# A fused RWKV attention and mixture-of-experts block: reordered first part, blends split between VectorE and ScalarE, one token table, row gathers three steps ahead

## The chip, the cores and the metric

The kernel runs on one core of a Trainium2 chip. The metric is the device time of one execution in microseconds (us). Beside the timed runs there is one profiled execution, whose trace gives the times of single instructions. The engines are called TensorE (PE in the profile; PEld are its weight loads), VectorE (DVE), ScalarE (ACT), GpSimd (POOL) and SyncE (SP). SyncE only issues DMAs here; GpSimd issues the indirect DMAs, which gather and scatter rows by index.

## The reference

The input x is 2 x 2048 tokens of 256 channels, fp32. It is normalised once, and two branches are added to it:

```python
xn  = layernorm(x)
out = x + attention(xn) + experts(xn)

def attention(x):                      # RWKV
    x = layernorm(x) * ln_g + ln_b
    last = x shifted by one token (0 ahead of the first)
    k = (x*mix_k + last*(1-mix_k)) @ Wk.T        # v, r alike
    num, den = num*td + exp(k)*v, den*td + exp(k)     # along time
    return (sigmoid(r) * num/(den + 1e-8)) @ Wo.T

def experts(x):                        # 8 experts, the best 2 of each token
    scores = relu(x @ Wr + br)
    w = softmax over the two best scores
    h = relu(x @ W1[e] + b1[e])        # 256 -> 1024
    return sum over the two of w[e] * (h @ W2[e] + b2[e])
```

## The kernel before, in words

The 4096 tokens are cut into 8 blocks of 512 (four to each batch row), a block into four tiles of 128 tokens. Everything after line 356 is written in the order in which each engine shall do it (`tc.manual_schedule()`), so the order of the calls in the source is the order of every engine's queue. Pools still decide when a buffer is free: `ps_a`, `ps_t`, `ps_h` and `ps_y` are PSUM pools of two buffers each.

*First part, lines 357 to 467.* For each block b, `stats(b)` (L180) computes mean and variance on VectorE and the reciprocal deviations on GpSimd (a power); `normed(b)` (L211) writes the normalised block x2, three quarters on VectorE and one on ScalarE, and SyncE stores it in a table in DRAM from which tokens are gathered later; `turned(b)` (L226) transposes the block on TensorE, and ScalarE evacuates each of the two channel halves twice, as x2T for the router and as xaT, scaled and shifted by ln_g and ln_b, for the attention. `scored(b)` (L246) multiplies by the router's weights, ScalarE copies the result out, and `routed(b)` (L259) transposes it into `sps`. `mix(n)` takes the next n blends from a generator (L266): once for a block VectorE computes dx = now - last, and then for k, v and r two instructions (one for each channel half) dx*mix + last. `some(n)` takes the next n of 48 projection outputs from another generator (L290): each is a 128x512 result of two fp32 matrix products in a `ps_a` buffer, which the profile shows as four matmul records, and ScalarE evacuates it into `kvr` (L304). `divisors` (L199) is another power on GpSimd.

*Routing, lines 468 to 695.* `best_two` (L336) finds the two experts of each token on VectorE. Two matmuls with ones and an upper triangle give prefix counts (`pre`, L482). A chain of small VectorE instructions (L497 to L554) turns these into a slot number for each token and expert, `pos`. There are 71 units of 128 slots; 64 of them form 32 pairs, 7 are single. The slots of one unit belong to one expert. To find the token of each slot, the positions are split into low and high parts, and for 8 chunks of 8 columns VectorE builds one-hot tables (L652 to L673): `oh_a` for the low part, `oh_b` for the high part, and `oh_t`, which is `oh_b` times the token's number less 2048. TensorE multiplies `oh_a` with both others, 16 matmuls a chunk, so that `inv` holds for each slot whether it is taken, and by which token. L683 to L692 turn this into two index tables: `frm`, the row to gather, and `into`, the row to scatter to, with empty slots sent to rows behind the last token. `experts_of_places` (L602) works out for each of 39 places (pairs and singles) which expert's weights it needs (`whose_i`), and the table `mine` for the gates. Between these steps `mix` and `some` calls are laid, so that TensorE has projections to do.

*Experts, lines 858 to 906.* There are 37 steps; each handles one place. `gather(s)` (L789) fetches the rows of its tokens, by one GpSimd DMA for each unit; `unnorm(s)` (L800) undoes a scaling of the rows and computes the gates; `turn(s)` (L814) transposes the rows; `first_product(s)` (L823) computes the 8 hidden chunks `hp`, with relu on ScalarE; `second_product(s, hs, i)` (L839) computes `yp`, adds the bias, multiplies by the gate, and scatters the result with an adding DMA on GpSimd. Weights are loaded by SyncE with expert numbers from `whose_i` (L773, L781). In step s the kernel issues the weights of steps s+1 and s+2, the gather of step s+2, then the first product of s, a part of the attention (`scans`, `gated`, `attended`), the transposes of s+1, the second product of s, and unnorm of s+2. The first 12 steps (SW = 12) add into a buffer `acc`, which starts as a copy of x; at the end of the twelfth, SyncE copies `acc` to the output (L906), and the remaining 25 steps add into the output itself. A last stage (L909 on) for two rare units runs only if they are needed.

Of the kernel before, what the change touches and what calls it, by code (L numbers as in the profile page):

```python
# [9 lines left out]
F32 = mybir.dt.float32  # L10
# [16 lines left out]
def rwkv_moe_block(  # L27
# [21 lines left out]
    nc = tc.nc  # L49
# [130 lines left out]
    def stats(b):  # L180
        def mk(nm, shape):
            return rpool.tile(shape, F32, bufs=1, name=f"{nm}_{b}")

        st = mk("st", [P, NS, 6])
        mv = mk("mv", [P, NS, 2])
        for i in range(NS):
            nc.vector.bn_stats(st[:, i, :], xts[b][:, i, :])
            nc.vector.bn_aggr(mv[:, i, :], st[:, i, :])
        mean, var = mv[:, :, 0], mv[:, :, 1]

        at = ts(b, NS)
        w = mk("w", [P, NS])
        nc.gpsimd.tensor_scalar(w, var, 1.0 + LN_EPS, LN_EPS * LN_EPS, ALU.mult, ALU.add)
        rrs[b] = rr_all[:, at]
        nc.gpsimd.tensor_tensor(rrs[b], w, power[:, 0:NS], ALU.pow)
        nc.gpsimd.tensor_scalar(ve_all[:, at], var, LN_EPS, 0.0, ALU.add, ALU.add)
        mrrs[b] = (mean, mk("mrr", [P, NS]))
# [28 lines left out]
    def turned(b):  # L226
        x2 = x2s[b]
        x2T = x2Ts[b] = rpool.tile([P, NC, TB], F32, tag="x2T", name=f"x2T_{b}")

        xaT = xaTs[b] = xa_pool.tile([P, NC, TB + 1], F32, name=f"xaT_{b}")  # L230
        if b % BPS == 0:
            nc.gpsimd.memset(xaT[:, :, 0:1], 0.0)
        else:
            nc.gpsimd.tensor_copy(xaT[:, :, 0:1], xaTs[b - 1][:, :, TB : TB + 1])
        for c in range(NC):
            tp = ps_t.tile([P, TB], F32, tag="pt", name=f"tp_{b}_{c}")
            for t in range(NS):
                nc.tensor.transpose(tp[:, ts(t, P)], x2[:, t, ts(c, P)], ident)
            nc.scalar.copy(x2T[:, c, :], tp)
            nc.scalar.activation(  # L240
                xaT[:, c, 1 : TB + 1], tp, AF.Identity, bias=vec(5, c), scale=vec(4, c)
            )

# [20 lines left out]
    blends = [[] for _ in range(NB)]  # L264

    def blender():  # L266
        for b in range(NB):
            now, last = xaTs[b][:, :, 1 : TB + 1], xaTs[b][:, :, 0:TB]

            dx = mixes.tile([P, NC, TB], F32, tag="dx", bufs=1, name=f"dx_{b}")  # L270
            nc.vector.tensor_tensor(dx, now, last, ALU.subtract)
            for i in range(3):
                m = mixes.tile([P, NC, TB], F32, tag="mix", name=f"mix{i}_{b}")
                for c in range(NC):
                    nc.vector.scalar_tensor_tensor(  # L275
                        m[:, c, :], dx[:, c, :], vec(1 + i, c), last[:, c, :],
                        ALU.mult, ALU.add,
                    )
                blends[b].append(m)
                yield  # L280
# [8 lines left out]

    def pieces():  # L290
        for b in range(NB):
            pool = kvr_pool if b < NB // 2 else kvr_late
            kvr[b] = pool.tile([P, 3, NC, TB], F32, tag="kvr", name=f"kvr_{b}")
            for i, (w, f, sign) in enumerate(
                ((wk_sb, AF.Exp, 1.0), (wv_sb, AF.Copy, 1.0), (wrr_sb, AF.Exp, -1.0))
            ):
                for o in range(NC):
                    m = blends[b][i]
                    p = ps_a.tile([P, TB], F32, tag="pa", name=f"p{i}_{b}_{o}")
                    for c in range(NC):  # L300
                        nc.tensor.matmul(  # L301
                            p, w[:, c, ts(o, P)], m[:, c, :], start=(c == 0), stop=(c == NC - 1)
                        )
                    nc.scalar.activation(kvr[b][:, i, o, :], p, f, scale=sign)  # L304
                    yield
# [50 lines left out]
    order = ctx.enter_context(tc.manual_schedule())  # L356
    stats(0)
    colp = ps_t.tile([P, n_rows], F32, tag="pt", name="colp")
# [10 lines left out]
    stats(1)  # L369
    normed(0)  # L370
    turned(0)


# [28 lines left out]
    token = count("token", NT, F16, base=-NTOK // 2, step=P, chan=1)  # L402
# [15 lines left out]
    stats(2)  # L418
    normed(1)
    scored(0)  # L420
    turned(1)
    nc.scalar.activation(td, cols[:, E * NH : E * NH + NC], AF.Exp)
    mix(3)
    routed(0)
    scored(1)
    normed(2)
    some(2)
    turned(2)
    routed(1)
    stats(3)  # L430
    stats(4)
    normed(3)
    some(2)
    scored(2)
    turned(3)
    divisors(0)
    routed(2)
    mix(3)
    some(2)
    scored(3)  # L440
    routed(3)
    stats(5)
    normed(4)
    some(2)
    turned(4)
    stats(6)
    normed(5)
    some(1)
    scored(4)
    turned(5)  # L450
    stats(7)
    normed(6)
    routed(4)
    some(1)
    scored(5)
    turned(6)
    divisors(1)
    normed(7)
    routed(5)
    some(1)  # L460
    scored(6)
    turned(7)
    mix(3)
    routed(6)
    some(1)
    scored(7)
    routed(7)
# [11 lines left out]
    some(4)  # L479
# [14 lines left out]
    some(2)  # L494
# [54 lines left out]
    )  # L549
    pos = rt("pos", (P, E, NT))  # L550
# [4 lines left out]
    some(6)  # L555
    mix(3)
    some(6)
    mix(1)

# [22 lines left out]
    mix(2)  # L582
# [18 lines left out]

    def experts_of_places():  # L602
# [15 lines left out]
        whose = rt("whose", (P, NW))  # L618
# [15 lines left out]
        nc.vector.tensor_copy(whose_i, whose)  # L634
        last = rt("last", (P, 2))
# [14 lines left out]
    inv = ps_y.tile([P, 2 * NU], F32, tag="py", name="inv")  # L650
    opool = routing.enter_context(tc.tile_pool(name="opool", bufs=3))
    for i0 in range(0, K * NT, CH):  # L652

        tables = []
        for nm, n, src, ramp2 in (("a", P, lo, lo_iota), ("b", NU, hi, hi_iota)):
            t = opool.tile([P, CH // 2, n, 2], F16, tag=f"oh_{nm}", name=f"oh_{nm}_{i0}")
            nc.vector.tensor_tensor(
                t,
                ramp2.unsqueeze(1).to_broadcast([P, CH // 2, n, 2]),
                src[:, i0 : i0 + CH].rearrange("p (a b) -> p a b", b=2).unsqueeze(2)  # L660
                .to_broadcast([P, CH // 2, n, 2]),
                ALU.is_equal,
            )
            tables.append(t)
        a, bq = tables
        bt_ = opool.tile([P, CH // 2, NU, 2], F16, tag="oh_t", name=f"oh_t_{i0}")
        t0 = i0 % NT
        nc.vector.tensor_tensor(
            bt_, bq,
            token[:, t0 : t0 + CH].rearrange("p (a b) -> p a b", b=2).unsqueeze(2)  # L670
            .to_broadcast([P, CH // 2, NU, 2]),
            ALU.mult,
        )  # L673
        mix((0, 0, 0, 1, 0, 1, 0, 2)[i0 // CH])
        for i in range(CH):
            for j, right in enumerate((bq, bt_)):
                nc.tensor.matmul(
                    inv[:, j * NU : (j + 1) * NU], a[:, i // 2, :, i % 2],
                    right[:, i // 2, :, i % 2],
                    start=(i0 + i == 0 and j == 0), stop=(i0 + i == K * NT - 1 and j == 1),  # L680
                )
        some((1, 1, 1, 1, 1, 2, 1, 0)[i0 // CH])
    invs = rt("invs", (P, 2, NU))  # L683
    nc.vector.tensor_copy(invs, inv.rearrange("p (a u) -> p a u", a=2))
    empty = rt("empty", (P, NU))
    nc.vector.tensor_tensor(empty, invs[:, 0, :], less, ALU.mult)
    row = rt("row", (P, NU))
    nc.vector.tensor_tensor(row, invs[:, 1, :], empty, ALU.subtract)
    into = const.tile([P, NU], I32, name="into")
    nc.vector.tensor_tensor(into, row, rest_row, ALU.add)  # L690
    frm = const.tile([P, NU], I32, name="frm")
    nc.vector.tensor_scalar_min(frm, into, float(NTOK - 1))  # L692
    mix(2)
    experts_of_places()
    routing.close()
    gpool = ctx.enter_context(tc.tile_pool(name="gpool", bufs=3, side="right"))
# [103 lines left out]
    def unnorm(s):  # L800

        gates[s] = []
        for i, g in enumerate(rows_of[s]):
            nc.vector.tensor_scalar(  # L804
                g[:, 0:C], g[:, 0:C], g[:, C + E : C + E + 1], None, ALU.mult
            )
        for i, g in enumerate(rows_of[s]):
            gm = small.tile([P, E], F32, tag=f"gm{i}", name=f"gm_{s}_{i}")
            nc.vector.tensor_tensor(gm, g[:, C : C + E], mine[:, seq[s], :], ALU.mult)
            gate = small.tile([P, 1], F32, tag=f"gate{i}", bufs=3, name=f"gate_{s}_{i}")  # L810
            nc.vector.tensor_reduce(gate, gm, AX.X, ALU.add)
            gates[s].append(gate)
# [26 lines left out]
    def second_product(s, hs, i):  # L839
# [7 lines left out]
        y = gpool.tile([P, C], F32, tag="y", bufs=5, name=f"y_{s}_{i}")  # L847
        nc.vector.tensor_tensor(y, yp, b2_sb, ALU.add)  # L848
        nc.vector.tensor_scalar(y, y, gates[s][i], None, ALU.mult)  # L849
# [9 lines left out]
    gather(1)  # L859
    load_first(0)  # L860
    load_second(0)
    load_first(1)
    some(6)
    unnorm(0)
    turn(0)
    some(2)
    unnorm(1)
    projecting.close()
    a1 = ctx.enter_context(tc.tile_pool(name="a1", bufs=1))
    hpool = ctx.enter_context(tc.tile_pool(name="hpool", bufs=2 * NH))  # L870
    turns = 0
    for s in range(NSTEP):
# [5 lines left out]
        if s + 2 < NSTEP:  # L878
            gather(s + 2)
# [13 lines left out]
        if b < NB:  # L893
            gated(b, o)
        adds = [second_product(s, hs, i) for i in range(len(units(seq[s])))]
# [5 lines left out]
        if s + 2 < NSTEP:  # L901
            unnorm(s + 2)
        if s == SW - 1:
# [9 lines left out]
    with tc.If(taken > 0):  # L913
# [6 lines left out]
        for s in range(NSTEP, NW):  # L920
# [3 lines left out]
            unnorm(s)  # L924
            turn(s)
# [42 lines left out]
```

## Time and profile before

| what | us |
|---|---|
| three timed runs | 665.69 to 669.6, median 667.3 |
| the profiled execution | 669.53 |
| its span, first to last instruction | 667.7 |
| TensorE busy | 637.4 (95%) |
| VectorE busy | 344.6 (52%) |
| ScalarE busy | 212.6 (32%) |
| GpSimd busy | 237.1 (36%) |
| first projection starts | 16.86 |
| last transpose of scores | 50.85 |
| first expert product starts | 123.04 |

A group row of the profile gives the line, engine, operation and tiles (result, then sources), the number of instructions; then busy time in us and the mean duration of one in ns; then the idle time ahead of them on their engine and what ended most of it. A timeline row gives start and duration in us, and in brackets the idle time before it with its releaser. Rows of digits are the span in 40 equal slices, in tenths; PEclk is the clock granted to TensorE in tenths of full speed. A SyncE row such as `117.85 0.40 SPq ... w` is the issue of a weight load, which lands some microseconds later (a median of 8.3 for the 1 MB loads).

### The profile page before, as it was taken

The page shows a single profiled execution, that of the slowest core. Times are in us where ns is not written, and L with a number is a line of the kernel's source. Part 1 is how long each engine was busy: PE and PEld are TensorE (multiplying, and loading weights), DVE is VectorE, ACT ScalarE, POOL GpSimd, SP SyncE. Part 2 cuts the span into 40 slices and gives each one's busy share as a digit, 9 for nine tenths or more (in the row PEclk, how much of TensorE's full clock was granted, in tenths as well). Part 3 has the DMA queues.
Part 4 walks back from the last instruction along what each step waited for, and adds up shares of the span by engine and source line. Part 5 has one row for each costly group of instructions (what it writes and reads, how often), then busy time and mean ns, then how long its engine had stood idle before and what let it go on. Part 6 is the DMA issues. An engine that isn't in the chain of part 4 may idle for free. (4 is left out here: it accounts for less than half of the span.)

```text
span 667.7 us, 9123 instructions
## 1 busy us (share of the span) xinstructions
PE 637.4 (95%) x3077; PEld 500.5 (75%) x3077; DVE 344.6 (52%) x779; ACT 212.6 (32%) x444; POOL 237.1 (36%) x206
## 2 busy tenths in 40 slices
PE   4999999899999999999989999999999999999993
PEld 2454454688888888887878888888888888888882
DVE  8988998446545547765587666422222121222110
ACT  4683323323332333332323333322223222222320
POOL 5551103034343354404355334343434433434211
PEclk9999999999999999999989999999999999999997
DMA  8548101876887886799677777777566776566621
GB/s 268 176 129 268 16 1 43 287 227 212 251 231 219 230 263 194 184 309 283 151 160 214 193 204 182 216 168 222 168 175 182 218 207 217 168 174 189 212 29 17
DMA packets 92408, 124.50 MB, mean 186 GB/s; under 512 B 15452, under 2 KB 80552, under 8 KB 92232
## 3 DMA queue, kind: packets, MB, share of 16 engines
q1 hardware_dynamic: 74368, 100.99, 46.3%
q0 software_dynamic: 17472, 22.86, 18.2%
q8 instruction: 25, 0.41, 0.3%
q14 instruction: 23, 0.19, 0.1%
q10 hardware_dynamic: 520, 0.05, 0.1%
HBM read 105.89 MB, written 26.38 MB: 198 GB/s over the span
## 5 line engine op out<-in xcount | busy, mean ns | idle before, releaser
L831 PE MATMUL hp<-xT,w 128*128 128x256 f32 (+1 forms) x1184 | 252.1, 369 | 2.3 <-DMA w<-in_L_ffn_W_dram 1.5
L835 ACT ACTIVATE h<-hp,b 128x256 f32<-128x256 f32 (+1 forms) x296 | 135.9, 459 | 349.2 <-PE hp L831 256.5
L844 PE MATMUL yp<-w,h 128*128 128x256 f32 x1104 | 246.1, 381 | 0.0
L831 PEld LDWEIGHTS hp<-xT,w 128*128 128x128 f32 x1184 | 199.2, 190 | 50.8 <-ACT h L835 16.6
L844 PEld LDWEIGHTS yp<-w,h 128*128 128x128 f32 x1104 | 208.6, 192 | 26.7
L853 POOL DMA_INDIRECT out_dram<-y,into x50 | 82.6, 1652 | 206.7 <-DVE y L849 129.5
L821 DVE COPY xT<-xp 128x512 f32<-128x512 f32 (+1 forms) x37 | 24.2, 655 | 148.2 <-PE xp L819 148.2
L793 POOL DMA_INDIRECT xg<-table,frm x69 | 77.8, 1127 | 55.7 <-DVE mix L275 34.9
L848 DVE TENSOR_TENSOR y<-yp,b 128x256 f32<-128x256 f32 x69 | 29.2, 423 | 115.3 <-PE yp L844 115.3
L853 POOL DMA_INDIRECT acc<-y,into x19 | 31.3, 1648 | 87.6 <-DVE y L849 51.2
L732 DVE RECIPROCAL dn<-dn 128x512 f32<-128x512 f32 x16 | 53.6, 3353 | 0.5
L304 ACT ACTIVATE kvr<-p 128x512 f32<-128x512 f32 x48 | 28.7, 599 | 54.9 <-PE p L301 54.9
L804 DVE TENSOR_SCALAR xg<-xg 128x256 f32<-128x256 f32 x69 | 22.3, 359 | 26.2 <-DMA xg<-table,frm 26.2
L275 DVE SCALAR_TENSOR_TENSOR mix<-dx,cols,xaT 128x512 f32<-128x512 f32 x48 | 33.3, 756 | 0.4
L301 PE MATMUL p<-mix,wk 128*128 128x512 f32 x64 | 30.4, 617 | 0.5 <-DVE mix L275 0.5
L301 PE MATMUL p<-mix,wv 128*128 128x512 f32 x64 | 29.5, 596 | 0.0
L301 PE MATMUL p<-mix,wr 128*128 128x512 f32 x64 | 29.3, 596 | 0.0
L741 PE MATMUL op<-wo,z 128*128 128x256 f32 x128 | 29.1, 380 | 0.0
L741 PEld LDWEIGHTS op<-wo,z 128*128 128x128 f32 x128 | 24.3, 190 | 3.6 <-ACT o_sb L744 0.3
L849 DVE TENSOR_SCALAR y<-y,gate 128x256 f32<-128x256 f32 x69 | 25.4, 369 | 2.4
L819 PE MATMUL xp<-ident,xg 128*128 128x128 f32 x138 | 21.7, 275 | 4.2 <-DVE xg L804 3.2
L819 PEld LDWEIGHTS xp<-ident,xg 128*128 128x128 f32 x138 | 17.0, 141 | 9.2 <-issue 1.9
(168 smaller groups left out, 365.4 us busy)
## 6 DMA issues: line engine op xcount, KB each, us to landing
w<-in_L_ffn_W_dram SPq DMA_DIRECT2D x74, 1024.0 KB, 8.3
b<-in_L_ffn_b_dram SPq DMA_DIRECT2D x37, 128.0 KB, 3.8
table<-x SPq DMA_DIRECT2D x8, 512.0 KB, 3.0
x<-in_L_attn_x_dram SPq DMA_DIRECT2D x7, 512.0 KB, 4.6
out_dram<-o_sb POOLq DMA_DIRECT2D x5, 512.0 KB, 6.1
acc<-o_sb POOLq DMA_DIRECT2D x3, 512.0 KB, 6.1
xg<-table,frm POOLq DMA_INDIRECT x69, 6.8
out_dram<-y,into POOLq DMA_INDIRECT x50, 6.7
```

Of the source, the lines that this page charges most:

```text
L275: nc.vector.scalar_tensor_tensor(m[:, c, :], dx[:, c, :], vec(1 + i, c), last[:, c, :], ALU.mult, ALU.add,)
L301: nc.tensor.matmul(p, w[:, c, ts(o, P)], m[:, c, :], start=(c == 0), stop=(c == NC - 1))
L304: nc.scalar.activation(kvr[b][:, i, o, :], p, f, scale=sign)
L732: nc.vector.reciprocal(dn, dn)
L741: nc.tensor.matmul(op, z[:, c, ts(t, P)], wo_sb[:, c, :], start=(c == 0), stop=(c == NC - 1))
L793: nc.gpsimd.indirect_dma_start(out=g, out_offset=None, in_=table, in_offset=bass.IndirectOffsetOnAxis(ap=frm[:, u : u + 1], axis=0), bound ...
L819: nc.tensor.transpose(xp[:, c, ts(i, P)], g[:, ts(c, P)], ident)
L831: nc.tensor.matmul(hp, w1_sb[:, c, ts(j, P)], xT[:, c, :], start=(c == 0), stop=(c == NC - 1))
L835: nc.scalar.activation(h[:, 0:n], hp, AF.Relu, bias=b1_sb[:, j : j + 1])
L844: nc.tensor.matmul(yp, hs[j][:, ts(i, P)], w2_sb[:, j, :], start=(j == 0), stop=(j == NH - 1))
L848: nc.vector.tensor_tensor(y, yp, b2_sb, ALU.add)
L853: return nc.gpsimd.indirect_dma_start(out=to, out_offset=bass.IndirectOffsetOnAxis(ap=into[:, u : u + 1], axis=0), in_=y, in_offset=None, ...
```

## The change

It has four parts.

*First part.* `stats` can be done for some of the four tiles. 25 matmuls of a 128x512 bf16 tile of zeros are put into TensorE's order (13, 4 and 8, `keep_warm`). `normed(0)` moves up, ahead of the transpose of the small vectors; block 0's evacuations change order (xaT before x2T) and its dx is taken in two halves. The calls of stats, normed, turned, scored, routed, mix and some are ordered anew; 15 projection outputs stand before the last transpose of scores, where 12 stood.

*Blends.* For blocks 3 to 7, ScalarE computes m = last*(1 - mix), one channel half after each projection output from the thirteenth on, and VectorE then does now*mix + m; these five blocks have no dx. A small table `unmixed` holds 1 - mix.

*One table of tokens.* The token's number is stored with an offset that keeps it from being zero: numbers 0 to 2047 as -2048 to -1, numbers 2048 to 4095 as 1 to 2048. So `oh_a` times `oh_t` alone tells empty slots (zero) from taken ones; each chunk has 8 matmuls instead of 16. `experts_of_places` moves ahead of the blends that followed `frm`, with its last part split off as `experts_later`; projections are laid between them, and `some(6)` before `unnorm(0)` becomes `some(4)`.

*Experts.* Three gathers are issued before the loop and gather(s+3) in step s; the rows have four buffers instead of three, and y has a pool of its own. The gates are split from `unnorm`. In the last step, the bias times the gate is prepared, and one VectorE instruction reads `yp`, multiplies and adds.

The core of the diff, with the reordered calls of the first part cut to their beginning:

```diff
@@ blends
+    NDX = 3
+    ahead = []
+
+    def preparer():
+
+        for b in range(NDX, NB):
+            for i in range(3):
+                m = mixes.tile([P, NC, TB], F32, tag="mix", name=f"mix{i}_{b}")
+                for c in range(NC):
+                    nc.scalar.activation(
+                        m[:, c, :], xaTs[b][:, c, 0:TB], AF.Copy, scale=unmixed[:, i, c : c + 1]
+                    )
+                    if c == NC - 1:
+                        ahead.append(m)
+                    yield
...
-            dx = mixes.tile([P, NC, TB], F32, tag="dx", bufs=1, name=f"dx_{b}")
-            nc.vector.tensor_tensor(dx, now, last, ALU.subtract)
+            if b < NDX:
+
+                dx = mixes.tile([P, NC, TB], F32, tag="dx", bufs=1, name=f"dx_{b}")
+                for c in (slice(0, 1), slice(1, NC)) if b == 0 else (slice(0, NC),):
+                    nc.vector.tensor_tensor(dx[:, c, :], now[:, c, :], last[:, c, :], ALU.subtract)
...
+                    by, other = dx, last
+                else:
+                    m = ahead.pop(0)
+                    by, other = now, m
                 for c in range(NC):
                     nc.vector.scalar_tensor_tensor(
-                        m[:, c, :], dx[:, c, :], vec(1 + i, c), last[:, c, :],
+                        m[:, c, :], by[:, c, :], vec(1 + i, c), other[:, c, :],
                         ALU.mult, ALU.add,
@@ pieces()
                     nc.scalar.activation(kvr[b][:, i, o, :], p, f, scale=sign)
+                    done += 1
+                    if done > NFIRST:
+                        next(preparing, None)
                     yield
@@ first part
+    keep_warm(13)
     stats(0)
+    stats(1, 0, 2)
+    normed(0)
...
-    stats(1)
-    normed(0)
+    stats(1, 2, NS)
+    keep_warm(4)
     turned(0)
...
+    mix(1)
...
-    stats(2)
     normed(1)
-    scored(0)
+    keep_warm(8)
+    some(2)
     turned(1)
@@ one-hot chunks
-            for j, right in enumerate((bq, bt_)):
-                nc.tensor.matmul(
-                    inv[:, j * NU : (j + 1) * NU], a[:, i // 2, :, i % 2],
-                    right[:, i // 2, :, i % 2],
-                    start=(i0 + i == 0 and j == 0), stop=(i0 + i == K * NT - 1 and j == 1),
-                )
-        some((1, 1, 1, 1, 1, 2, 1, 0)[i0 // CH])
+            nc.tensor.matmul(
+                inv, a[:, i // 2, :, i % 2], bt_[:, i // 2, :, i % 2],
+                start=(i0 + i == 0), stop=(i0 + i == K * NT - 1),
+            )
+        some(SOME[i0 // CH])
...
     nc.vector.tensor_scalar_min(frm, into, float(NTOK - 1))
+    experts_of_places()
     mix(2)
-    experts_of_places()
+    some(2)
+    mix(1)
+    some(2)
+    mix(1)
+    experts_later()
     routing.close()
-    gpool = ctx.enter_context(tc.tile_pool(name="gpool", bufs=3, side="right"))
+    gpool = ctx.enter_context(tc.tile_pool(name="gpool", bufs=4, side="right"))
@@ second_product()
+        y = ypool.tile([P, C], F32, tag="y", name=f"y_{s}_{i}")
+        if s == NSTEP - 1:
+            nc.vector.scalar_tensor_tensor(y, yp, gates[s][i], b2g[i], ALU.mult, ALU.add)
+        else:
+            nc.vector.tensor_tensor(y, yp, b2_sb, ALU.add)
+            nc.vector.tensor_scalar(y, y, gates[s][i], None, ALU.mult)
@@ experts
     gather(0)
     gather(1)
+    gather(2)
...
-    some(6)
+    some(4)
     unnorm(0)
     turn(0)
     some(2)
+    gate(0)
     unnorm(1)
+    gate(1)
...
-        if s + 2 < NSTEP:
-            gather(s + 2)
+        if s + 3 < NSTEP:
+            gather(s + 3)
```

## The prediction, made before the changed kernel was run

> **What bounds the kernel now.** I read the page first: the busy row of TensorE, the granted clock, the costliest groups, the list of waits. The page's chain that ended last has two pieces at the very end of the span, so it carries nothing here.
>
> ```profile
> PE   4999999899999999999989999999999999999993
> PEclk9999999999999999999989999999999999999997
> L304 ACT ACTIVATE kvr<-p 128x512 f32<-128x512 f32 x48 | 28.7, 599 | 54.9 <-PE p L301 54.9
> L275 DVE SCALAR_TENSOR_TENSOR mix<-dx,cols,xaT 128x512 f32<-128x512 f32 x48 | 33.3, 756 | 0.4
> ```
>
> TensorE is full except in the first slice, one slice in the middle (slice 21, about 334 us) and the last; its row sums to 637.4 of 667.7 us. So time can be won only where TensorE idles or runs slowly, and where its own instructions go. ScalarE waits 54.9 us for projections: it has room. VectorE never waits for blends (0.4). The timeline of TensorE shows the gaps:
>
> ```profile
> 9.21 1.97 PE L238 MATMUL tp<-ident,x 128*128 128x128 f32 x8 [1.84 <-ACT x L221]
> 16.86 4.81 PE L301 MATMUL p<-mix,wk 128*128 128x512 f32 x8
> ...
> 51.02 3.60 PE L301 MATMUL p<-mix,wk 128*128 128x512 f32 x8
> 54.45 3.60 PE L301 MATMUL p<-mix,wv 128*128 128x512 f32 x8
> ...
> 123.04 7.24 PE L831 MATMUL hp<-xT,w 128*128 128x256 f32 x32 [1.50 <-DMA w<-in_L_ffn_W_dram]
> ```
>
> From 51.02 to 54.45 are two projection outputs, 1.716 us each. At 16.86 the same eight matmuls take 4.81 instead of 3.60: a cold array. The first expert product starts at 123.04.
>
> ```profile
> 315.20 0.41 PE L819 MATMUL xp<-ident,xg 128*128 128x128 f32 x2 [0.69 <-DVE xg L804]
> 316.12 0.44 PE L819 MATMUL xp<-ident,xg 128*128 128x128 f32 x2 [0.51 <-DVE xg L804]
> 335.48 0.41 PE L819 MATMUL xp<-ident,xg 128*128 128x128 f32 x2 [1.56 <-DVE xg L804]
> 336.30 0.48 PE L819 MATMUL xp<-ident,xg 128*128 128x128 f32 x2 [0.41 <-DVE xg L804]
> 336.58 8.76 PE L844 MATMUL yp<-w,h 128*128 128x256 f32 x32
> ```
>
> ```profile
> 303.76 1.61 POOL L853 DMA_INDIRECT out_dram<-y,into  x1 [20.99 <-DMA out_dram<-acc]
> 307.80 1.09 POOL L793 DMA_INDIRECT xg<-table,frm  x1 [0.30 <-PE yp L844]
> ```
>
> The bracket is the idle time before a row and what ended it. Rows gathered late stop TensorE four times, 3.17 us in all, and after the last the second product takes 8.76 where its neighbours take 7.07: 1.69 more. The GpSimd rows say why: the scatters of step 12 wait 20.99 us for the copy of acc into the output, and the gather of step 15 stands behind them in GpSimd's order.
>
> **The change, part by part.** The built order of the changed kernel gives each engine's queue; I laid the queues end to end with durations of the profile above.
>
> *First part, to the last transpose of scores (sp_7).* The 25 matmuls on zeros: 13 stand before the first transpose, 4 before the transposes of block 0, 8 before the first projections. Taken at the records' pace (a 128x512 fp32 projection record lies 0.43 us apart, the bf16 one is not in this trace; at most that), they end by 7.7, 9.7 and 12.7, each ahead of the inputs of what follows, so they cost nothing; if that cover were gone, 25×0.43 = 10.7 us. VectorE takes the blend of block 0 sooner: the first half of dx waits till 11.5 for the zero column, which GpSimd writes behind the statistics' powers (3.2 us each); two halves of dx and of the blend later the first projection can start at 13.65, against 16.86. It runs warm and saves 1.2 more. From there on ScalarE and VectorE, not TensorE, set the pace: ScalarE evacuates in order, 2.75 us a turned block, 0.60 an output, 0.27 a score, and outputs have two PSUM buffers. The last block's normalisation waits for its power behind divisors on GpSimd until 44.7, the third blend of block 2 comes at 47.95, and sp_7 ends at 57.0 against 51.18. By then 15 outputs are done, not 12: 3×1.716 = 5.15. Net +0.67. The early gain is lost in the queues; sp_7 as early as 55.0 is possible if the orders mesh better.
>
> *Blends on ScalarE.* Thirty multiplies of 128x512 go to ScalarE. The rows near: 717 ns for dn (same shape, from SBUF, one pointer, line 730), 585 and 794 for the two evacuations of turned blocks. I take 717; ends 585 and 794. VectorE loses five dx of 1298 ns, 6.5 us; its two halves of a blend stay 1.36.
>
> ```profile
> L730 ACT ACTIVATE dn<-den,den_eps 128x512 f32<-128x512 f32 x16 | 11.5, 717 | 6.4 <-DVE den L709 6.4
> L271 DVE TENSOR_TENSOR dx<-xaT 128x1024 f32<-128x1024 f32 x8 | 10.4, 1298 | 0.1
> ```
>  The Trainium skill, "ScalarE: Activation LUTs", section "Rules for kernel authors", speaks against this: multiplies and adds belong on VectorE, which does them faster. By that rule the change is a loss, 21.5 us of ScalarE for 6.5 of VectorE. By the rows it costs no time: an output's evacuation and its multiply are 0.60+0.72 = 1.32 a projection of 1.716, and ScalarE has 54.9 us of waiting there. I follow the rows. In the one-hot loop two chunks and a blend take VectorE 2×1.46+1.36 = 4.28, while TensorE's two half chunks and two outputs take 0.57+3.43 = 4.0: a near tie, for which I count waits of 0.85.
>
> *One table.* 64 matmuls fewer: a chunk of sixteen takes 0.57 (87.09 to 87.65), half of it 0.285, eight chunks save 2.3 us of TensorE. The rows after it (five VectorE operations, 1.25 us, 1.35 before) are a tie.
>
> *Experts sooner.* This is the step that costs. VectorE now does 5.9 us of small operations (109.98 to 115.9 before) right behind the token rows (1.25+0.2), then 0.72 for the first half of blend 2 of block 6, on which the next projection waits: 8.07. Before, two blends came first. TensorE has two outputs queued meanwhile, 3.43 us. So 4.65 us idle. What is gained by it is small: in the built order the first weight load of SyncE waits for the last table of experts and for ScalarE's last multiply, so weights land 120 to 122, just in time, and the 1.50 at 123.04 goes.
>
> Then the array after the gap. The Trainium skill, "TensorE: Matmul & The Clock Gate", section "Why this matters for your kernels", says a gap beyond about 3 us returns the array to its low clock. The trace has harsher and softer rows: 1.56+0.41 us at 335 was followed by 1.69 lost, 1.50 at 121.5 by nothing.
>
> ```profile
> 334.00:337.00 3.00, 1.11 (x6) 0.82 (x7) 1.62 (x7) 0.32 (x1) 2.52 (x2) 0.93 0.99 346
> 337.00:341.00 4.00, 4.00 (x13) 3.27 (x12) 3.96 (x7) 0.72 (x1) 3.26 (x3) 0.63 0.61 103
> ```
>
> The columns are busy times of TensorE, weight loads, VectorE, ScalarE, GpSimd, then the granted clock: 0.63 in the 4 us behind the stall. For 4.65 both say cold: +1.7, as at 336.58. For the gap of 2.65 at 11.0 to 13.65 the rule says none and the row up to 1.7; ScalarE bounds that stretch, so I take none. Without the cold array the sum below is 1.7 less.
>
> *From sp_7 to the first expert product:* 33 outputs ×1.716 = 56.6, half chunks 2.3, prefix counts 0.24, transposed rows 0.45, seams of 0.07 at eight chunks 0.5, waits 0.85, the hinge 4.65, cold array 1.7: 67.3. 57.0+67.3 = 124.3 against 123.04: +1.3.
>
> *Rows three steps ahead.* The gather of step 15 is now issued in step 12, ahead of the blocked scatters; that of 16 comes at 307.8, lands 6.8 later (before 320, when it is used), 17 at about 327.6, landing 334.4, used from 338. The four waits and their cold array go: 3.17+1.69 = 4.86. The extra gather ahead is GpSimd's, 2×1.13 us before step 0, where it waits for nothing and delays only its own scatters; a fourth buffer of rows lets it be. Behind the gap nothing else is late: weights and outputs' PSUM stand as before.
>
> *Last step.* One operation from PSUM in place of 656.59 (0.42) and 657.05 (0.35): one goes with its hand-over, 0.46 from the first's start to the second's. The prepared bias is off the path, a few small operations behind transposes.
>
> Gates apart from unnorm, and the two halves of dx, cost nothing: VectorE's row on the page stands at 2 tenths in the main loop.
>
> **Sum.** +1.3 −4.86 −0.46 = −4.0. Span 667.7 → 663.7; the profiled execution was 669.53, so 665.5. That execution stood 2.2 above the median of the three runs, 667.3 (665.69 to 669.6); against the median: 663.3. A change of 0.5%, 3.3 us, is about what a measurement of this kernel can tell from none.
>
> **Rivals.**
> *The front works.* If the first part meshes (sp_7 at 55.0) and the hinge leaves the array warm, hp_0 comes 3.7 sooner: −7.7, 659.6. For it: the first projection really is 3.2 us sooner, and 1.50 us of gap left no trace at 123.04. Against it: 5.9 us of VectorE work cannot be covered by 3.43 of TensorE. Chance 0.2.
> *The rows are late anyway.* If GpSimd's queue, not the order of one gather, is what is late (its scatters of steps 12 to 14 come in a burst at 303.76), the mid stall moves to a later step: +1.3−0.46, 668.1. For it: each gather takes 6.8 to land and shares the queue with two scatters of 1.65. Against it: before, the gathers of steps 17 on were in time from the same burst. Chance 0.15.
> *ScalarE becomes the bound of the projections* (the slower side). Place: 57 to 120, where each output's evacuation is followed by its multiply and two PSUM buffers hold TensorE to ScalarE's pace. Price: if a multiply of the shifted, 513-wide source takes x, each of 30 outputs is late by x+0.60−1.716. It decides from x = 1.25 us, where 30×0.13 = 4.0 eats the gain; at twice the nearest row, 1.43, 30×0.32 = 9.5 makes 672.8. Against it: no SBUF source of that shape takes more than 0.72. Chance 0.1.
> *It does not do what it says:* weights sooner is such a case already, taken at nothing above.
>
> **How the numbers follow.** The forecast, 663.3, has 0.52, its own range 661 to 666; 0.03 is left for both sides. The range reaches to the first two rivals: 658.5 to 668.5. Below 664.0 lie the first rival and some 0.7 of the forecast's case: faster 0.58; within 0.5%: the rest of it and the second rival, 0.31; slower: 0.11.
>
> **What would show it.** First projection at about 13.7 with records of a warm 3.4 to 3.6; sp_7 near 57; a wait of TensorE for mix of 4 to 5 us near 104 to 110, followed by slow records; ScalarE's multiplies of 0.7 us; hp_0 near 124; no wait for rows around 315 and 335; one VectorE operation before the last scatter. I am wrong if TensorE waits on PSUM outputs behind ScalarE between 57 and 120, if waits for rows move to another step, or if the hinge is covered.

## The result, and the profile after

The changed kernel takes 664.92 us (median of 20 runs, 664.53 to 665.95) where the kernel before, run beside it, takes 668.62 (665.69 to 669.71); the ratio is 0.9954, with a 95% interval of 0.9945 to 0.9964. Its profiled execution took 665.95, the longest of its runs, with a span of 664.3.

From the page of the changed kernel, the rows of TensorE and of the granted clock, and the groups of the outputs' evacuation, of the new multiplies on ScalarE (from the groups by form) and of the blends that use them:

```profile
PE   7989997999999999999999999999999999999993
PEclk9999997999999999999999999999999999999998
```

```profile
L342 ACT ACTIVATE kvr<-p 128x512 f32<-128x512 f32 x48 | 28.7, 599 | 41.4 <-PE p L339 40.8 <-ACT mix L285 0.6
L285 ACT ACTIVATE mix<-xaT,unmixed 128x512 f32<-128x512 f32 x30 | 21.4, 714 | 0.0
L310 DVE SCALAR_TENSOR_TENSOR mix<-xaT,cols,mix 128x512 f32<-128x512 f32 x30 | 22.0, 779 | 7.0 <-ACT mix L285 6.9
```

The dent in slice 21 is gone, and a new one stands in slice 7 (100 to 116 us), where the granted clock falls too. A multiply on ScalarE takes 714 ns. VectorE's blends wait 6.9 us for such multiplies, in three places; TensorE waits behind none of them. TensorE's timeline, first part and way to the first expert product:

```profile
13.74 3.70 PE L339 MATMUL p<-mix,wk 128*128 128x512 f32 x8 [2.42 <-DVE mix L310]
...
57.01 0.27 PE L273 MATMUL sp<-ident,s 128*128 128x128 f32 x1
...
101.08 3.67 PE L339 MATMUL p<-mix,wv 128*128 128x512 f32 x8
108.82 6.73 PE L339 MATMUL p<-mix,wr 128*128 128x512 f32 x8 [4.07 <-DVE mix L310]
115.38 3.60 PE L339 MATMUL p<-mix,wk 128*128 128x512 f32 x8
...
126.12 7.16 PE L914 MATMUL hp<-xT,w 128*128 128x256 f32 x32
```

The first projection is 3.1 us sooner and warm; the last transpose of scores ends at 57.28 (before: 51.18), with three more outputs done, worth 5.15: 0.95 later. At 108.82 is the hinge: 4.07 us of waiting for a blend, then two outputs in 6.73 instead of 3.67. VectorE's queue shows what the blend stands behind; its small operations fill the time from the first of these rows to the second:

```profile
102.33 0.16 DVE L681 COPY limits<-fcum 128x8 f32<-128x8 f32 x1
...
107.93 4.06 DVE L310 SCALAR_TENSOR_TENSOR mix<-xaT,cols,mix 128x512 f32<-128x512 f32 x6
```

The window behind it (columns as in the prediction's windows):

```profile
110.00:118.00 8.00, 8.00 (x15) 3.23 (x14) 3.84 (x8) 3.01 (x5) 1.90 (x2) 0.69 0.22 52
```

The last three numbers are granted clock, DMA share and GB/s: 0.69 over these 8 us, and 0.53 over the slow records alone (108.80 to 115.40). In the middle, TensorE and GpSimd's queue:

```profile
317.36 0.60 PE L902 MATMUL xp<-ident,xg 128*128 128x128 f32 x4
317.79 7.07 PE L927 MATMUL yp<-w,h 128*128 128x256 f32 x32
...
335.15 0.60 PE L902 MATMUL xp<-ident,xg 128*128 128x128 f32 x4
335.58 7.07 PE L927 MATMUL yp<-w,h 128*128 128x256 f32 x32
```

```profile
305.55 1.62 POOL L939 DMA_INDIRECT out_dram<-y,into  x1 [19.61 <-DVE dn L812]
...
309.35 1.09 POOL L874 DMA_INDIRECT xg<-table,frm  x1 [0.30 <-issue]
```

The scatters still wait 19.61 us. The bracket names a VectorE operation here and the copy of acc in the kernel before; the scatter comes 15.75 and 15.86 us after the issue of that copy (305.55 after 289.80; in the kernel before, 303.76 after 287.90), so I read it as the copy again. No transposed rows wait, and the second product is back at 7.07. The last operations, and the last scatter of the kernel before:

```profile
653.72 0.48 DVE L932 SCALAR_TENSOR_TENSOR y<-yp,gate,b2g 128x256 f32<-128x256 f32 x1 [2.97 <-PE yp L927]
654.48 1.55 POOL L939 DMA_INDIRECT out_dram<-y,into  x1 [1.90 <-DVE y L932]
```

```profile
657.68 1.55 POOL L853 DMA_INDIRECT out_dram<-y,into  x1 [1.90 <-DVE y L849]
```

So the two spans differ by: first expert product 126.12 against 123.04, +3.08; from there to the last scatter 528.36 against 534.64, −6.28, of which 1.09−0.76 = 0.33 lies between the start of the last VectorE operations and that scatter, and 5.95 before them; behind the last scatter −0.2. Together −3.4.

### The profile page after: what moved, and what is told of

Its sections match the earlier page's. It is cut to its first block, busy times and chain, and to the rows that moved or that the text cites. A ratio compares the mean times of both kernels' runs of the same rounds, so it can differ in the third digit from the quotient of the medians.

```text
span 664.3 us, 9082 instructions
## 1 busy us (share of the span) xinstructions
PE 638.8 (96%) x3038; PEld 498.2 (75%) x3038; DVE 338.0 (51%) x777; ACT 230.4 (35%) x474; POOL 233.1 (35%) x207
## 5 line engine op out<-in xcount | busy, mean ns | idle before, releaser
L874 POOL DMA_INDIRECT xg<-table,frm x69 | 75.2, 1090 | 45.1 <-PE p L339 24.3
L342 ACT ACTIVATE kvr<-p 128x512 f32<-128x512 f32 x48 | 28.7, 599 | 41.4 <-PE p L339 40.8
L339 PE MATMUL p<-mix,wr 128*128 128x512 f32 x64 | 32.7, 650 | 4.5 <-DVE mix L310 4.1
L339 PEld LDWEIGHTS p<-mix,wr 128*128 128x128 f32 x64 | 12.7, 207 | 19.5 <-issue 17.0
L310 DVE SCALAR_TENSOR_TENSOR mix<-xaT,cols,mix 128x512 f32<-128x512 f32 x30 | 22.0, 779 | 7.0 <-ACT mix L285 6.9
L339 PEld LDWEIGHTS p<-mix,wk 128*128 128x128 f32 x64 | 11.5, 190 | 16.6 <-issue 12.2
```

The lines of the kernel that those rows point to most:

```text
L339: nc.tensor.matmul(p, w[:, c, ts(o, P)], m[:, c, :], start=(c == 0), stop=(c == NC - 1))
L874: nc.gpsimd.indirect_dma_start(out=g, out_offset=None, in_=table, in_offset=bass.IndirectOffsetOnAxis(ap=frm[:, u : u + 1], axis=0), bound ...
```

## The experiments

Ratios are to the kernel before, run on the same chip at the same time; the changed kernel's is 0.9954. The kernels ran on several chips, on which the kernel before had medians of 667.64 to 668.62, so that a difference of two medians is the less certain figure where both are given. The theory is that of the prediction: a loss at the hinge and in the reordered first part, a gain in the middle. Its rivals stand with each run.

**The hinge.** In the first kernel the blends come first again:

```diff
-    experts_of_places()
     mix(2)
+    experts_of_places()
```

> The changed kernel with one call moved: the next two blends stand ahead of the experts of places on VectorE again. Theory A (the hinge: the projection behind the one-hot chunks waits 4.07 us for its blend and then runs cold, 6.73 instead of 3.60): both go, less about 0.5 for the blend after the small operations, so the first expert product starts near 119.5 instead of 126.12 and the time is 6 to 7 us less, 658 to 659. Theory B (the weights are what is late next: 5.2 us lie between the issue behind the gates' table and the first product): the product starts at 122 to 123 with a wait for w, the time is 3 to 4 less. Theory C (the gap is only moved): no change, 665.

Measured: 661.08 us, ratio 0.9889 (0.9871 to 0.9908). TensorE's timeline:

```profile
100.92 3.67 PE L339 MATMUL p<-mix,wv 128*128 128x512 f32 x8
104.43 3.60 PE L339 MATMUL p<-mix,wr 128*128 128x512 f32 x8
...
120.74 7.24 PE L914 MATMUL hp<-xT,w 128*128 128x256 f32 x32 [1.60 <-DMA w<-in_L_ffn_W_dram]
```

Both theories are half right. The stall and the cold records are gone as A says (without the last wait the product would start at 119.14), and then the weights are late, as B says, by 1.60. The time came out as B says: the hinge cost about 4 us net (3.8 by the medians, 4.4 by the ratios).

In the second, zeros are multiplied where TensorE would stand still:

```diff
     experts_of_places()
+    keep_warm(18)
     mix(2)
```

(The tile of zeros moves to the constants' pool, so that it still exists there.)

> The changed kernel with 18 more matmuls on zeros (0.22 us each when warm, 4.0 us together) in TensorE's order where it waits for the blend. The stall of 4.07 stays. Theory A (the 6.73 us of the records behind the gap are a cold array): they take 3.6 to 3.7, the first expert product starts near 123.0, the time is 3.0 less, 662. Rival (the records are slow because VectorE writes blends and ScalarE reads at the same time, or for another cause than the gap): they stay at 6.7, the time stays at 665.

Measured: 663.21 us, ratio 0.9920 (0.9905 to 0.9936).

```profile
102.00 4.05 PE L405 MATMUL warm<-idle 128*128 128x512 bf16 x18
105.89 3.60 PE L339 MATMUL p<-mix,wv 128*128 128x512 f32 x8
109.73 3.67 PE L339 MATMUL p<-mix,wr 128*128 128x512 f32 x8 [0.25 <-issue]
```

The zeros' 4.05 us take the place of the idle time, the records behind them take 3.67, and from 102.00 to the first expert product are 21.98 us, where the changed kernel needs 25.04 from the same point. The granted clock over the records from 109.70 to 113.30 is 1.00. So the slow records came from the gap, and the cold array was a cost of its own, 3.06 between these two profiles; the times show 1.7 by the medians, 2.3 by the ratios.

**Rows three steps ahead.** Undone in the changed kernel:

```diff
-    gather(2)
...
-        if s + 3 < NSTEP:
-            gather(s + 3)
+        if s + 2 < NSTEP:
+            gather(s + 2)
```

> The changed kernel with gathers two steps ahead, as before; the four buffers of rows stay. Theory A (the gather of step 15 behind the scatters that wait for the copy of acc is the whole middle loss): the waits around steps 15 and 16 return, the time is 5.7 us more, 670.6. Rival (the fourth buffer or another part removed the waits): no change, 665.

Measured: 674.0 us, ratio 1.0075 (1.0055 to 1.0095). TensorE and GpSimd in the middle:

```profile
323.13 1.09 PE L902 MATMUL xp<-ident,xg 128*128 128x128 f32 x4 [5.41 <-DVE xg L884]
324.01 8.23 PE L927 MATMUL yp<-w,h 128*128 128x256 f32 x32
```

```profile
311.00 1.61 POOL L939 DMA_INDIRECT out_dram<-y,into  x1 [25.09 <-DVE y L935]
312.91 1.58 POOL L939 DMA_INDIRECT out_dram<-y,into  x1 [0.30 <-issue]
314.80 1.09 POOL L874 DMA_INDIRECT xg<-table,frm  x1 [0.30 <-issue]
```

The mechanism returns as expected, but larger, 9.1 us by the medians and 8.1 by the ratios: the scatters stand 25.09 us, not 20.99. What holds them 5.4 us longer than in the changed kernel (305.55) with the copy issued at the same time, 289.5, was not settled.

Done alone in the kernel before:

```diff
+    gather(2)
...
-            gather(s + 2)
+            gather(s + 3)
...
-    gpool = ctx.enter_context(tc.tile_pool(name="gpool", bufs=3, side="right"))
+    gpool = ctx.enter_context(tc.tile_pool(name="gpool", bufs=4, side="right"))
```

> The kernel before with only this part: three gathers ahead, four buffers of rows. Theory A (the parts add up): the time is 5.7 us less than before, 0.9915 of it, and the start of the first expert product stays at 123.0 to 123.2. Rival (the extra gather ahead of the first step delays rows there, or the middle gain needs the other parts): less than 3 us gained.

Measured: 674.13 us, ratio 1.0081 (1.0064 to 1.0098): slower. From the waits, and from TensorE's timeline:

```profile
POOL xg L793 <- DVE mine L644: 44.4, 1, 44.4
```

```profile
125.94 0.66 PE L819 MATMUL xp<-ident,xg 128*128 128x128 f32 x2 [8.95 <-DVE xg L804]
128.68 0.69 PE L819 MATMUL xp<-ident,xg 128*128 128x128 f32 x2 [2.07 <-DVE xg L804]
129.16 6.29 PE L301 MATMUL p<-mix,wr 128*128 128x512 f32 x8
```

The middle's gain is there (528.89 us from first expert product to last scatter, with no wait for rows), but the first gather waits for the table `mine` and starts at 118.41, where it started at 108.33 before. A gather reads nothing of `mine`. In the built program this wait is for memory: the pool of rows, a fourth buffer larger and with y still in it, lies over `whose` and other tiles that the experts of places use, and `mine` is made from `whose`. The next kernel takes y out of it, into a pool of five buffers of its own:

```diff
-        y = gpool.tile([P, C], F32, tag="y", bufs=5, name=f"y_{s}_{i}")
+        y = ypool.tile([P, C], F32, tag="y", name=f"y_{s}_{i}")
```

> The kernel before with three gathers ahead and four buffers of rows, and with y in a pool of its own, so that the pool of the gathered rows is no larger than before. Theory A (in the earlier try the first gathers waited for the table of gates only because their fourth buffer lay over its memory): that wait is gone, the first expert product starts at 123 to 124, no wait for rows stands around 315 and 335, the time is 5.7 us less than before, 0.9915 of it. Rival (the third gather ahead itself delays the first rows): the product starts later than 126 and less than 3 us is gained.

Measured: 663.76 us, ratio 0.9932 (0.9915 to 0.9950); from the first expert product to the last scatter are 528.95 us.

```profile
122.52 7.24 PE L831 MATMUL hp<-xT,w 128*128 128x256 f32 x32 [1.58 <-DMA w<-in_L_ffn_W_dram]
```

Theory A holds: the wait for `mine` is gone, and that stretch is 5.69 us shorter than before. The times show 4.5 of the 5.7. This one part does by itself at least what the whole change does.

**The first part.** The old order, without the zeros, in the changed kernel:

```diff
-    keep_warm(13)
     stats(0)
-    stats(1, 0, 2)
-    normed(0)
...
-    stats(1, 2, NS)
-    keep_warm(4)
+    stats(1)
+    normed(0)
     turned(0)
...
-    mix(1)
...
+    some(3)
+    mix(1)
     some(5)
```

(In the last cut stands the list of calls, in the order of before.)

> The changed kernel with the first part in the order of before and without the matmuls on zeros (12 outputs ahead of the last transpose of scores; a blend and three outputs more behind it). Theory A (the first part is paced by queues of ScalarE and VectorE, and its new order is worth nothing or loses the 0.95 us that the two profiles show): the first expert product starts between 125 and 126.2, the time is 664 to 665. Rival (the earlier, warm first projection carries through): 2 to 3 us more, 667 to 668.

Measured: 664.07 us, ratio 0.9933 (0.9914 to 0.9952).

```profile
99.97 3.67 PE L339 MATMUL p<-mix,wv 128*128 128x512 f32 x8
107.70 5.37 PE L339 MATMUL p<-mix,wr 128*128 128x512 f32 x8 [4.06 <-DVE mix L310]
...
123.64 7.17 PE L902 MATMUL hp<-xT,w 128*128 128x256 f32 x32
```

Theory A by the time, and somewhat more: 0.85 us less by the medians, 1.4 by the ratios, with intervals that overlap. In this profile the first expert product starts at 123.64, 2.5 sooner than in the changed kernel; 1.11 of it is there when the one-hot chunks end (99.97 against 101.08), and 1.36 is the cold array, which takes 5.37 here behind a gap of the same length, not 6.73. The rival is out: the sooner first projection carried nothing through. One pair of profiles does not measure the first part closely: the last transpose of scores starts at 50.18 to 51.64 in the six profiles with the old order and at 56.88 to 58.55 in the eight with the new one. The means are 51.07 and 57.57, 6.50 apart, where three more outputs are worth 5.15.

Then the zeros alone (`keep_warm` calls left out):

> The changed kernel without its 25 matmuls on zeros. Theory A (ScalarE's and VectorE's queues pace the first part, so a cold start of TensorE is absorbed): the transposes and the first projection take 1 to 2 us more, the last transpose of scores stays within 0.5 of 57.0, the time within 0.7 of the changed kernel, 664.3 to 665.6. Rival (the warm start carries through): 1.5 to 3 us more, 666.5 to 668.

Measured: 665.1 us, ratio 0.9964 (0.9950 to 0.9978), the same as the changed kernel.

```profile
14.39 5.86 PE L339 MATMUL p<-mix,wk 128*128 128x512 f32 x8 [3.41 <-DVE mix L310]
...
57.69 0.27 PE L273 MATMUL sp<-ident,s 128*128 128x128 f32 x1
```

The first projection is slow, 5.86 instead of 3.70, and started 0.65 later, and the last transpose of scores stands 0.68 later, a little over the 0.5 of the expectation and inside the spread of the other profiles. The 2.16 us are absorbed. (The granted clock reads 1.00 over these records, as it does over the 4.81 at 16.86 in the kernel before; that the array was cold at these two places is read from the durations alone.)

**Blends on ScalarE.** All on VectorE again:

```diff
-    NDX = 3
+    NDX = NB
```

> The changed kernel with all blends on VectorE alone, dx for all eight blocks, nothing on ScalarE. Theory A (VectorE has no room between 57 and 110, so four dx of 1.3 us there push the blend at the hinge back): the first expert product starts 4 to 5.5 us later, 130 to 131.6, the time is 669 to 670.5. Rival (the rule that multiplies belong on VectorE holds here; the share of ScalarE brings nothing): within 1 us of 665, or less than that since ScalarE's last multiplies no longer hold VectorE up.

Measured: 670.31 us, ratio 1.0029 (1.0013 to 1.0046), 5.4 us more than the changed kernel by the medians and 5.0 by the ratios. Theory A by the time. The first one-hot chunk, in the changed kernel and here, and two later outputs here:

```profile
84.45 0.44 PE L755 MATMUL inv<-oh_t,oh_a 128*128 128x71 f16 x8 [1.19 <-DVE oh_t L747]
```

```profile
87.36 0.64 PE L755 MATMUL inv<-oh_t,oh_a 128*128 128x71 f16 x8 [3.87 <-DVE oh_t L747]
...
105.32 3.67 PE L339 MATMUL p<-mix,wv 128*128 128x512 f32 x8
113.06 5.37 PE L339 MATMUL p<-mix,wr 128*128 128x512 f32 x8 [4.07 <-DVE mix L310]
```

VectorE waits for nothing from 57.84 to 104.05 here. The first chunk waits 3.87 instead of 1.19 for it, the last is done 4.2 us later (105.32 against 101.08), and the wait at the hinge is the same. The first expert product starts at 129.00, only 2.9 later and sooner than expected, as the cold array takes 5.37 here and not 6.73; so the two profiled executions differ by 3.2 us, less than the medians.

**One table.** Both products again, the second's result used:

```diff
-            nc.tensor.matmul(
-                inv, a[:, i // 2, :, i % 2], bt_[:, i // 2, :, i % 2],
...
+            for j, right in enumerate((bq, bt_)):
+                nc.tensor.matmul(
+                    inv_[:, j * NU : (j + 1) * NU], a[:, i // 2, :, i % 2],
```

> The changed kernel with both products again for each one-hot chunk, 16 matmuls instead of 8; the second product's result alone is used. Theory A (TensorE bounds the chunks, one output and eight matmuls 1.72+0.29 and a seam, so that halving the products saved its full 2.3): the outputs there stand 2.36 apart instead of 2.03 to 2.08 and the time is 2.0 to 2.3 more, 667. Rival (VectorE bounds the chunks, 1.46 and half a blend 0.68, and the saving was hidden): less than 0.7 more.

Measured: 667.88 us, ratio 1.0003 (0.9991 to 1.0014), 3.0 more than the changed kernel (3.3 by the ratios). Theory A, with somewhat more than its 2.3. The outputs of the chunks:

```profile
96.63 1.96 PE L339 MATMUL p<-mix,wr 128*128 128x512 f32 x4
98.99 1.96 PE L339 MATMUL p<-mix,wk 128*128 128x512 f32 x4
101.35 1.96 PE L339 MATMUL p<-mix,wk 128*128 128x512 f32 x4
```

They stand 2.36 apart; in the changed kernel 2.00 to 2.16:

```profile
96.92 1.96 PE L339 MATMUL p<-mix,wk 128*128 128x512 f32 x4
...
99.00 1.96 PE L339 MATMUL p<-mix,wk 128*128 128x512 f32 x4
```

**What is late next.** With the blends first, the gates' table and the last small operations moved behind the first rows, and the weights ahead of their bias:

```diff
-    whose = rt("whose", (P, NW))
+    whose = const.tile([P, NW], F32, name="whose")
...
     mix(1)
-    experts_later()
     routing.close()
...
     some(2)
+    experts_later()
     gate(0)
```

(`e_iota`, `last`, `fcum` and `pairs` move to the constants' pool too, and in `load_first` the load of w1 ahead of that of b1.)

> The kernel with the two blends ahead of the experts of places, and the gates' table and the last small operations moved behind the first transposed rows; the small tables that they read lie in the constants' pool, and the weights of the first product are issued ahead of its bias. Theory (after the hinge, what is late next is the first weights: 1.60 us of waiting, as their load stands behind those operations and the bias): the load is issued 1.3 to 1.8 us sooner, the wait goes, the first expert product starts at 119.0 to 119.4 instead of 120.74, the time is 1.4 less, 659.6. Rival (the load waits for the last blend, not for these operations): no change, 661.

Measured: 661.32 us, ratio 0.9891 (0.9870 to 0.9911): no gain. The load was issued sooner, at 114.50, 12.66 behind the end of the one-hot chunks, where it had been 14.48, but TensorE got its weights 6.4 us after the issue, at 120.95, where it had been 5.3. Why the load took longer is open.

```profile
114.50 0.41 SPq L857 DMA_DIRECT2D w<-in_L_ffn_W_dram  x1
...
120.95 7.16 PE L913 MATMUL hp<-xT,w 128*128 128x256 f32 x32 [0.89 <-DMA w<-in_L_ffn_W_dram]
```

Then with the old first part as well, and last the same without the weights' move:

> The changed kernel with the first part in the order of before (no matmuls on zeros), the two blends ahead of the experts of places, and the first weights ahead of the gates' table and of the bias. Theory (the new first part loses about 1 us, the hinge 4 us and a cold array; both are mended here): the first expert product starts at 118.6 to 119.6, the time is 659 to 660.3, under that of the kernels with one of the two mended (661.1 and 664.1). Rival (the two gains overlap, since the product waits for its weights in any case): 661 to 661.5.

> The changed kernel with the first part in the order of before and the two blends ahead of the experts of places, but with the gates' table and the bias ahead of the first weights again. Theory (once first part and hinge are mended, the first weights are what is late: with them sooner the first expert product started at 117.59 without a wait): it starts at 118.8 to 119.5 behind a wait for w of 1.2 to 1.8, the time is 658.5 to 659.2 against 657.3. Rival (the weights' order is worth nothing, as it was on top of the new first part, 661.3 against 661.1): 657.3, and the gain beyond expectation is the first part's alone.

Measured: 657.33 us, ratio 0.9848 (0.9830 to 0.9866), the fastest kernel here, and 659.25 us, ratio 0.9860 (0.9840 to 0.9880). SyncE's first weight load and TensorE's first expert product, of the one and the other:

```profile
112.18 0.41 SPq L845 DMA_DIRECT2D w<-in_L_ffn_W_dram  x1
...
117.59 7.09 PE L901 MATMUL hp<-xT,w 128*128 128x256 f32 x32
```

```profile
114.71 0.40 SPq L847 DMA_DIRECT2D w<-in_L_ffn_W_dram  x1
...
119.71 7.24 PE L902 MATMUL hp<-xT,w 128*128 128x256 f32 x32 [1.26 <-DVE den L778]
```

The wait of 1.26 is there without the move and gone with it. (The engine named had not begun that work; the product follows the load by 5.0 us, and I read it as the weights.) By the medians the move is worth 1.9 us, by the ratios 0.8, with intervals that overlap; with the new first part it was worth nothing. The first part's old order is worth more than the expectation said: between the kernels with the weights' move 2.9 us by the ratios and 4.0 by the medians, without it 1.9 and 1.8. That part of it which needs no weights can be read where the one-hot chunks end: 99.52 and 100.22 in these two kernels, 101.84 and 100.92 in the two with the new order.

## Why the prediction was right

The time was forecast at 663.3, 4.0 less than before; measured are 3.4 us between the spans and 3.7 between the medians. The measured time itself is 1.6 above the forecast; 1.3 of it is that the forecast stood on the median of three runs, 667.3, where 20 runs have 668.62. Step by step:

- *First part, +0.67:* 0.95 in the two profiles. That it is paced by the queues of ScalarE and VectorE was right: a cold start was absorbed, and the sooner first projection brought nothing. Its order loses 1.4 to 2.9 us by the ratios of the three pairs in which it was undone (0.9 to 4.0 by the medians). In the first pair 1.36 us of that lie in the cold array, in the other two a part in the weights; but the mean of the profiles above, 6.50 less 5.15, is 1.35 as well, so this term was too kind.
- *Zeros, 0:* right.
- *ScalarE's multiplies, 717 ns and hidden:* 714 ns, with 40.8 us of ScalarE's waiting left, and hidden from TensorE, though VectorE waited 6.9 us for them. The rule of the Trainium skill ("ScalarE: Activation LUTs", "Rules for kernel authors") to leave multiplies to VectorE would have cost 5.0 to 5.4 us here, since VectorE has no room in that stretch. The prediction did not give this part its own price; that it gains this much was not seen.
- *One table, −2.3:* −3.0.
- *Experts sooner, 4.65 of waiting and 1.7 of cold array:* 4.07, and 3.06 in the profiled run (6.73 against 3.67). In three other profiles with the same gap the cold array cost 1.70. The profiled run of the changed kernel was its longest, 1.03 over the median; that the cold array made it so would fit, but was not shown. This is the mis-sized term. Between +1.3 and the measured +3.08 for the first expert product, the cold array is 1.36, the first part 0.28, the wait at the first one-hot chunk 0.34 (1.19, in the sum 0.85 for all) and the hinge's wait −0.58; some 0.4 is spread over small seams.
- *Weights no sooner, just in time:* right; they were next in line by 1.3 to 1.6 us as soon as the hinge was mended.
- *Rows three ahead, −4.86:* −5.95. The waits and the slow second product were 3.17+1.69 as counted. The two steps with the waits lost 0.42 and 0.41 more than that; there the transposes of a pair come in two pieces, which I read as the cause. The rest is 0.20 at step 17 and 0.07 in the first step. Another 0.28, gained at step 4, is lost again at step 9, where TensorE waits 0.35 us for ScalarE in the changed kernel.
- *Last step, −0.46:* −0.33; the one operation from PSUM takes 0.48, not 0.42.

So the loss ahead of the experts was 1.8 us larger than forecast and the gain behind it 1.1 us larger. The mechanisms were right, but that the sum came so near is in part luck: the two errors have opposite signs. Of the rivals, "the front works" did not come, since the hinge was not covered (with the blends first most of it does, 661.08 against its 659.6); "the rows are late anyway" and "ScalarE becomes the bound" did not come.

## What to carry to other kernels

A block of small operations put ahead of a blend on VectorE costs TensorE the time by which it exceeds the outputs already queued (here 4.07 us), and then a cold array on top (1.70 to 3.06 us); ask what TensorE has in hand at that point, and move the block behind the next blends if it isn't enough. A deeper prefetch needs memory, and a pool that grows can lie over tiles that are still in use: look in the built program at what the first transfer waits for before judging the idea by its time. Being ready earlier at the front was worth nothing here, where the queues behind it set the pace.

## What the runs showed that was not expected

Behind a gap of 4.05 to 4.13 us in the stream of fp32 records TensorE was cold each time, but for different lengths: two outputs took 5.37 us in three profiles, 6.09, 6.30 and 6.73 in the others, where warm ones take 3.6 to 3.7. The granted clock over these records is 0.67 in the three and 0.59, 0.57 and 0.53 in the others. At the first projections, gaps of 0.93, 1.75 and 2.42 us gave warm records (3.70, clock 1.00), and gaps of 2.07 (twice) and 2.28 cold ones (5.40, clock 0.67). The Trainium skill ("TensorE: Matmul & The Clock Gate", "Part 1: The HAM clock gate (the "warmup" mystery)") says that activity is counted in windows of about 3.4 us that run freely, so that the point of change depends on the phase. The spread of the loss, 1.70 to 3.06 us behind the same gap, agrees with it; that a gap near 2 us went both ways would too, though the page's limit for gaps is about 3 us. The phase itself is in no row of the profile.

The copy of acc into the output, issued at the same time in two kernels (289.5 and 289.8), let the scatters behind it go 5.4 us later in one of them, the run with rows two steps ahead: 21.5 us after the issue, where the thirteen other profiles have 15.4 to 17.0. The cause is open.
